# Projecting a cross-attention's context in four 32-row tiles of the array: keys and values of a Perceiver layer on Trainium2

## The chip, the cores and the metric

The kernel runs on one core of a Trainium2 chip, as one launch. The core has a matrix engine (TensorE; PE in the profile, with PEld for its weight loads), a vector engine (DVE), an activation engine (ACT), GpSimd (POOL) and an engine that issues transfers (SP). Matrix products are written into PSUM, which has eight banks of 128 partitions × 512 float32 numbers; the other engines read them from there. The metric is the device time of one execution in microseconds (us), lower is better. Times of a kernel are given as the median of several runs; the profile is of one further execution with a time of its own.

## The reference, cut to what matters

The program computes two layers of a Perceiver-like network on `x` (4 batches × 256 tokens × 256 channels) with a context `ctx` (4 × 4096 keys × 192 channels), all in float32:

```python
x = x + L0_xattn(layernorm(x), ctx, mask, Wq, Wk, Wv, Wo)     # the block that is changed
x = x + L0_attn(layernorm(x), ...)
x = x + L0_ffn(layernorm(x), ...)
x = x + L1_xattn(layernorm(x), ctx, ...)
x = x + L1_attn(layernorm(x), ...)
x = x + L1_ffn(layernorm(x), ...)
```

The block in question is an attention with 16 heads of 16 channels:

```python
q = (xn @ Wq).reshape(4, 256, 16, 16)      # Wq 256 x 256
k = (ctx @ Wk).reshape(4, 4096, 16, 16)    # Wk 192 x 256
v = (ctx @ Wv).reshape(4, 4096, 16, 16)    # Wv 192 x 256
p = softmax(where(mask, q . k / sqrt(16), -big))   # 256 x 4096 per batch and head
out = (p . v).reshape(4, 256, 256) @ Wo
```

The change touches the two products `ctx @ Wk` and `ctx @ Wv`: 4 × 4096 rows, 192 channels in, 256 out each.

## The kernel before, in words

`l0_xattn` works in 16 units, u = 4 × batch + g: four groups g of four heads for each of four batches. Four heads lie in the four 32-row groups of a tile (16 channels, then a row for the maximum, a row for the mask, padding). Keys `kts` and values `vs` each have two tiles, one for each pair of groups (`gp`): while one pair is read, the other is refilled. Between them lie 8 refills of keys and 8 of values (4 batches × 2 pairs), each in four chunks of 1024 keys.

A unit has 16 steps (`step`, lines 424 to 478). A step does two things side by side: for unit u it weighs 256 keys (`s`), and for the unit that is 18 steps (`LEAD`) ahead it looks for the largest score over a stretch of 512 keys (`a`). It has two half steps of two heads each. On TensorE a half step runs two `weigh(0)` matmuls (line 444, bank `ps_s`, 256 columns), two scores for the maximum (line 458, `ps_a`, 512 columns), two `weigh(1)`, and then `sums` (line 406), four matmuls of exponentials with values into `o_ps`. ACT takes the exponentials out of `ps_s` (line 469), DVE the maxima out of `ps_a` (line 473). `sums` uses the exponentials of the step before. In the profile every float32 matmul shows as two LDWEIGHTS and two MATMUL records.

PSUM: `x0_acc` holds one bank (`o_ps`), `x0_ring` the other seven, which `bank(name)` hands out in turn. A half step takes four: two `ps_s` and two `ps_a`. A bank can be written again when the engine that reads it is done.

The projections are generators, advanced by the loop at the end of `l0_xattn` after a step (line 508). `projections[u]` projects keys in even units and values in odd ones, for units 0 to 13. Keys advance by a chunk after steps 0, 4, 8 and 12 of their unit; values by half a chunk after every second step. Before the loop's first weighing there are 18 steps with `a` only, and in these the first refills (batch 0, pair 0) are done: keys up to step 3, values (`first_values`) half a chunk after each of steps 9 to 17, as far as there are any.

A keys chunk (`keys`, lines 288 to 309): a context chunk of 768 KB, laid out as 128 channels × 1024 keys and below it the other 64 channels as two halves of 512 keys, is loaded by `context_keys` (line 233) on SP's queue. Two banks get 512 keys each: two matmuls over 128 rows (line 295) and two over 64 rows, in the array's upper and lower half (line 298). ACT copies both banks to SBUF (line 301), and eight transfers of 64 KB spread the heads' rows into `kts` (line 305). Half a values chunk (`values`, lines 311 to 336): here the context is the stationary operand, with 128 keys to a matmul, and the weights (128 columns of one pair of groups) are streamed: four matmuls over 128 rows (line 322) and four over 64 rows (line 325) into two banks, in the order of two groups per 128 keys; ACT copies each bank (line 335) into `vs`.

Weights: `l0_xattn_weights` loads `x0_wk` by three transfers on ACT's queue (`load_kk`, lines 242 and 244) ahead of the first context chunk (line 200); `others`, called at step 3 of the first 18, loads `x0_wv`, the x rows of batches 1 to 3 (line 210) and `x0_wo` on SP. `tokens(b)` normalises a batch's x (`row_norm`, lines 120 to 134, DVE) and transposes it (line 347); `queries(u)` projects the queries of a unit, `with_largest(u)` puts the maxima into the query tile, `finish(u)` divides by the sum (`attn_finish`, lines 165 to 174) and after the fourth group adds the output projection.

The order on each engine follows the program text closely, but the framework that builds the program puts some instructions elsewhere: the trace shows the normalisation of batches 1 to 3 (line 127) at 29 to 36 us, long before the units that use it.

Of the kernel before, what the change touches and what calls it, by code (L numbers as in the profile page):

```python
# [11 lines left out]
F32 = mybir.dt.float32  # L12
# [9 lines left out]
P = 128  # L22
B, S, D = 4, 256, 256
# [96 lines left out]
def row_norm(c, pool, name, b):  # L120

    v = c.nc.vector
    xn = pool.tile([P, 2, D], F32, tag=name, name=name)
    mv = pool.tile([P, 2, 2], F32, tag="nr_mv", name="nr_mv")
    for i in range(2):
        st = pool.tile([P, 6], F32, tag="nr_st", name="nr_st")
        v.bn_stats(st, c.x[:, 2 * b + i, :])
        v.bn_aggr(mv[:, i, :], st)
    rs = newton_rsqrt(c, pool, mv[:, :, 1], 2)
    for i in range(2):  # L130
        v.tensor_scalar(
            xn[:, i, :], c.x[:, 2 * b + i, :], mv[:, i, 0:1], rs[:, i : i + 1], ALU.subtract, ALU.mult
        )
    return xn
# [60 lines left out]

def l0_xattn_weights(c, pool):
    w = Ctx()
    w.wk = load_kk(c, pool, "x0_wk", c.nc.scalar)
    w.ctxT = [pool.tile([P, 1536], F32, tag="ctxT0", name="ctxT0")]
    c.nc.scalar.dma_start(w.ctxT[0], c.a["ctxT"][0, 0])  # L200
    w.mu = pool.tile([64, S], U8, tag="mu", name="mu")
    c.nc.sync.dma_start(w.mu, c.a["gmask"].rearrange("b (a k) -> (b a) k", k=S))
    w.wq = load_k(c, pool, "x0_wq")

    def others():

        w.wv = load_kk(c, pool, "x0_wv")
        xv = c.a["x"].rearrange("b (t p) d -> p (b t) d", p=P)
        for i in range(2, NB, 2):
            c.nc.sync.dma_start(c.x[:, i : i + 2, :], xv[:, i : i + 2, :])  # L210
# [18 lines left out]
def context_keys(c, pool, b, c4, queue=None):  # L229


    t = pool.tile([P, 1536], F32, tag="ctxT", name="ctxT")
    (queue or c.nc.sync).dma_start(t, c.a["ctxT"][b, c4])
# [12 lines left out]


def l0_xattn(c, w):
# [5 lines left out]

    nc, tc = c.nc, c.tc
    W = 17
    LEAD = 18
    with ExitStack() as es:  # L260
# [5 lines left out]
        def bank(name):  # L266
            return ring.tile([P, 512], F32, tag="mm", name=name)

        kts, vs, mexps = [], [], []
        for i in range(2):  # L270
# [7 lines left out]
        w.ctxT += [context_keys(c, two, 0, 1), context_keys(c, two, 0, 2, nc.scalar)]  # L278
# [4 lines left out]
        def mask(b, gp):  # L283
            for i in range(2):
                nc.sync.dma_start(kts[gp][17:P:32, i, :], c.mrow[b].partition_broadcast(4))

        def keys(b, gp):

            gs = slice(gp * P, (gp + 1) * P)
            first = (b, gp) == (0, 0)  # L290
            for c4 in range(4):
                ctxT = w.ctxT.pop(0) if w.ctxT else context_keys(c, two, b, c4)
                pss = [bank("ps_k0"), bank("ps_k1")]
                for j, ps in enumerate(pss):
                    nc.tensor.matmul(ps, w.wk[:, 0, gs], ctxT[:, j * 512 : (j + 1) * 512], start=True, stop=False)
                for j, ps in enumerate(pss):
                    hs = slice(64 * j, 64 * j + 64)
                    nc.tensor.matmul(ps, w.wk[hs, 1, gs], ctxT[hs, 1024:1536], start=False, stop=True)  # L298
                ks = two.tile([P, 2, 512], F32, tag="ks", name="ks")
                for j, ps in enumerate(pss):  # L300
                    nc.scalar.copy(ks[:, j, :], ps)  # L301
                for i in range(2):
                    for h in range(4):
                        r = 64 * i + 16 * h
                        ((nc.scalar, nc.gpsimd)[i] if first else nc.sync).dma_start(
                            kts[gp][32 * h : 32 * h + 16, i, c4 * 1024 : (c4 + 1) * 1024],
                            ks[r : r + 16].rearrange("p j n -> p (j n)"),
                        )
                yield

        def values(b, gp):
            v = vs[gp]
            gs = slice(gp * P, (gp + 1) * P)
            for c4 in range(4):
                ctxT = context_keys(c, two, b, c4)
                for i0 in (0, 2):
                    pss = [bank("ps_v0"), bank("ps_v1")]
                    for i in (i0, i0 + 1):
                        ks = slice((i - i0) * P, (i - i0 + 1) * P)
                        for j, ps in enumerate(pss):  # L320
                            k0 = j * 512 + i * P
                            nc.tensor.matmul(ps[:, ks], ctxT[:, k0 : k0 + P], w.wv[:, 0, gs], start=True, stop=False)  # L322
                        for j, ps in enumerate(pss):
                            hs = slice(64 * j, 64 * j + 64)
                            nc.tensor.matmul(  # L325
                                ps[:, ks],
                                ctxT[hs, 1024 + i * P : 1024 + (i + 1) * P],
                                w.wv[hs, 1, gs],
                                start=False,
                                stop=True,  # L330
                            )
                    for j, ps in enumerate(pss):
                        n0 = (8 * c4 + 4 * j + i0) * 8
                        o = v[:, n0 * W : (n0 + 16) * W].rearrange("p (n d) -> p n d", d=W)
                        nc.scalar.copy(o[:, :, 0:16], ps[:, 0 : 2 * P].rearrange("p (n d) -> p n d", d=16))  # L335
                    yield

        xnTs = {}

        def tokens(b):  # L340

            xn = row_norm(c, two, "xn", b)
            xnT = two.tile([P, 2, S], F32, tag="xnT", name="xnT")
            ps = bank("ps_t")
            for k in range(2):
                for i in range(2):
                    nc.tensor.transpose(
                        ps[:, k * S + i * P : k * S + (i + 1) * P], xn[:, i, k * P : (k + 1) * P], c.ident
                    )
            nc.scalar.copy(xnT.rearrange("p k n -> p (k n)"), ps)  # L350
            xnTs[b] = xnT
# [66 lines left out]
        def finish(u):  # L418
            b, g = divmod(u, 4)
            on = one.tile([P, S], F32, tag=f"on{g}", name=f"on{g}")  # L420
            attn_finish(c, two, ring, o_pss.pop(u)[:, :S], on)
            ons.append(on)
            if g == 3:
                add_projected(c, ring, b, ons, w.wo)
                ons.clear()
# [58 lines left out]
        for t in range(-LEAD, n):  # L484
            if t < 0:
                i = t + LEAD
                if i in (0, 2):
                    next(first_keys, None)
                if i == 3:
                    w.others()  # L490
                    for j in range(2):
                        nc.gpsimd.memset(kts[1][:, j, :], 1.0)
                if i > 8:
                    next(first_values, None)
            u, kp = divmod(t, 16)
            ua, ka = divmod(t + LEAD, 16)
            if ua < 16 and ka == 0 and ua > 0:
                queries(ua)
            if ua < 15 and ka == 8 and ua % 4 == 3:
                tokens(ua // 4 + 1)  # L500
            step((u, kp) if t >= 0 else None, (ua, ka % 2, ka // 2) if ua < 16 else None)
            if ua < 16 and ka == 15:
                with_largest(ua)
            if u in projections:
                steps, nb, ngp = projections[u]
                if kp == 0 and u % 2 == 0:
                    mask(nb, ngp)
# [1445 lines left out]
def _arrays(i):  # L1953
# [11 lines left out]
    for m in range(P):  # L1965
# [18 lines left out]
        "x": i["x"],  # L1984
        "ctx": i["ctx_768"],
        "ctxT": ctxT,
        "gmask": i["mask_BxS2_bf1"].view(np.uint8),
        "cols": cols,
        "sel": sel,
        "x0_wq": _pad_cols(i["L0_xattn_Wq"], 16, 16, 32),  # L1990
        "x0_wk": i["L0_xattn_Wk"],
        "x0_wv": i["L0_xattn_Wv"],
# [74 lines left out]
```

## Time and profile before

| what | value |
|---|---|
| runs | 2672.73, 2675.63, 2672.99 us; median 2672.99 |
| profiled execution | 2677.02 us, its span 2674.9 us |
| mean granted TensorE clock over the span | 0.929 |
| TensorE busy | 2420.3 us, 90% of the span |
| DVE busy, ACT busy | 1618.9 us (61%), 1095.0 us (41%) |
| layer 0's cross-attention | 0 to about 1236 us |
| of this, TensorE busy from 250 to 1180 us | 908.7 of 930 us |
| first key projection, first max reduce, first o_ps | 10.41, 24.87, 103.22 us |

How to read it. A group line names the source line, the engine, the operation, what is written and what is read, their shapes and how many there were; behind the bar the sum of their durations (us), the mean of one (ns), and the idle time of the engine just before them with what ended it. A timeline line has the start (us), the duration, the engine and the line, and a count where neighbouring instructions of the same kind are drawn together. Durations of matmuls overlap, since they are pipelined: four matmuls side by side in the array show their full latency each. What a stretch of matmuls costs is read from where the next one starts. "32\*128 32x256" is an operand of 32 rows (a quarter of the array's rows) × 128 columns, with 256 columns streamed through it.

### The profile page before, as it was taken

To read this page: it belongs to the slowest core of one execution; us is meant where nothing else is said; L and a number is where in the kernel's file an instruction comes from. 1 tells how busy PE (TensorE), PEld (TensorE's weight loads), DVE (VectorE), ACT (ScalarE), POOL (GpSimd) and SP (SyncE) were. 2 spreads that over 40 slices of the span, in tenths; PEclk is the share of its full clock that TensorE was granted. 3 is DMA by queue.
4 is the path that set the end of the run, shared out by engine and by line. 5 is a ranking of instruction groups with operands and counts; after the bars stand their busy time and mean duration, and the time that the engine had idled before them with its cause. 6 is when DMAs were issued, how large, how long until landed. Compare 5 with 4: busy or idle time off the path is not lost. (4 is left out here: it accounts for less than half of the span.)

```text
span 2674.9 us, 47755 instructions
## 1 busy us (share of the span) xinstructions
PE 2420.3 (90%) x19345; PEld 1419.5 (53%) x19345; DVE 1618.9 (61%) x3881; ACT 1095.0 (41%) x1913; POOL 179.1 (7%) x202
## 2 busy tenths in 40 slices
PE   8999999999999999999768989888999898984896
PEld 4445454545545454544435544466776777453554
DVE  6655655565565655561784440898798892735554
ACT  1355555555455555556111211555555562010221
POOL 3000000000000000000030000001010011412000
PEclk7899999999999999999888999799999999996876
DMA  7221213121221212100100012210303012100110
GB/s 197 76 53 58 61 50 80 38 73 45 62 56 55 63 37 73 45 2 1 43 1 1 5 47 67 79 60 20 99 22 97 6 50 96 55 0 16 33 24 8
DMA packets 63186, 130.78 MB, mean 49 GB/s; under 512 B 11584, under 2 KB 38912, under 8 KB 62512
## 3 DMA queue, kind: packets, MB, share of 16 engines
q1 hardware_dynamic: 61344, 123.73, 16.4%
q8 instruction: 154, 2.52, 0.4%
q10 hardware_dynamic: 1104, 2.88, 0.4%
q0 software_dynamic: 512, 1.05, 0.2%
q14 instruction: 72, 0.59, 0.1%
HBM read 97.12 MB, written 5.34 MB: 38 GB/s over the span
## 5 line engine op out<-in xcount | busy, mean ns | idle before, releaser
L473 DVE TENSOR_REDUCE mx<-ps_a 128x1 f32<-128x512 f32 x1024 | 658.3, 686 | 436.1 <-PE ps_a L458 436.1
L469 ACT ACTIVATE e<-ps_s 128x512 f32<-128x512 f32 x1024 | 555.8, 594 | 382.5 <-PE ps_a L458 356.5
L458 PE MATMUL ps_a<-kt,qa 32*128 32x512 f32 x2048 | 636.2, 653 | 1.9 <-DMA kt<-ks 0.8
L444 PE MATMUL ps_s<-qb,kt 32*128 32x256 f32 x4096 | 585.9, 401 | 0.0
L444 PEld LDWEIGHTS ps_s<-qb,kt 32*128 32x128 f32 x4096 | 348.7, 184 | 212.4 <-issue 94.2
L406 PE MATMUL o_ps<-e,v 128*32 128x256 f32 x4096 | 327.6, 391 | 0.0
L1152 PEld LDWEIGHTS ps_w<-diag,e 128*128 128x128 f32 x2048 | 238.8, 197 | 23.5 <-issue 21.5
L1152 PE MATMUL ps_w<-diag,e 128*128 128x128 f32 x2048 | 244.5, 281 | 0.4 <-POOL diag L1139 0.4
L458 PEld LDWEIGHTS ps_a<-kt,qa 32*128 32x128 f32 x2048 | 220.6, 186 | 20.9 <-DVE mx L473 7.8
L1109 DVE MAX8 cand<-sc 128x8 f32<-128x128 f32 x1024 | 212.2, 275 | 8.7 <-ACT sc L1097 8.7
L406 PEld LDWEIGHTS o_ps<-e,v 128*32 128x32 f32 x4096 | 81.0, 108 | 239.5 <-issue 229.5
L1133 DVE SCALAR_TENSOR_TENSOR e<-sc,top,e 128x1024 f32<-128x1024 f32 x128 | 159.1, 1279 | 28.5 <-ACT e L1124 28.5
L1124 ACT ACTIVATE e<-sc,neg 128x1024 f32<-128x1024 f32 x128 | 143.1, 1147 | 33.3 <-PE ps_w L1152 29.1
L1097 ACT COPY sc<-ps_s 128x1024 f32<-128x1024 f32 x128 | 126.3, 1007 | 41.9 <-PE ps_s L1088 39.6
L1166 PEld LDWEIGHTS ps_c<-cx,wT 128*128 128x128 f32 x512 | 86.1, 196 | 27.2 <-ACT wT L1160 11.3
L1166 PE MATMUL ps_c<-cx,wT 128*128 128x193 f32 x512 | 97.1, 341 | 1.9 <-ACT wT L1160 1.9
L335 ACT COPY v<-ps_v 128x256 f32<-128x256 f32 x128 | 41.4, 375 | 137.0 <-PE ps_v L325 137.0
L322 PE MATMUL ps_v<-x_wv,ctxT 128*128 128x128 f32 x512 | 92.8, 305 | 0.0
L322 PEld LDWEIGHTS ps_v<-x_wv,ctxT 128*128 128x128 f32 x512 | 69.4, 195 | 35.3 <-DVE mx L473 21.8
L1088 PE MATMUL ps_s<-kt,q 32*128 32x512 f32 x512 | 85.4, 647 | 0.0
L889 POOL MEMSET s_low<- 128x128 f32 x2 | 0.3, 206 | 1241.1 <-DVE x L188 1241.1
L301 ACT COPY ks<-ps_k 128x512 f32<-128x512 f32 x64 | 34.4, 589 | 111.4 <-PE ps_k L298 97.7
(403 smaller groups left out, 2735.6 us busy)
## 6 DMA issues: line engine op xcount, KB each, us to landing
ctxT<-in_ctxT SPq DMA_DIRECT2D x78, 768.0 KB
kt<-ks SPq DMA_DIRECT2D x352, 64.0 KB
cx<-in_ctx SPq DMA_DIRECT2D x16, 768.0 KB
x_w<-in_x_w SPq DMA_DIRECT2D x2, 1024.0 KB
qk<-rot SPq DMA_DIRECT2D x8, 256.0 KB
a_qk<-qk SPq DMA_DIRECT2D x16, 128.0 KB
ctxT<-in_ctxT ACTq DMA_DIRECT2D x2, 768.0 KB
x<-in_x SPq DMA_DIRECT2D x4, 256.0 KB
```

What stands on the lines that cost most here:

```text
L322: nc.tensor.matmul(ps[:, ks], ctxT[:, k0 : k0 + P], w.wv[:, 0, gs], start=True, stop=False)
L406: nc.tensor.matmul(o_pss[u][32 * h : 32 * h + 32, :S], vs[g // 2][:, c0 : c0 + 32], ew[h][:, n % 2, :], start=(n == 0), stop=(n == GT - 1),)
L444: nc.tensor.matmul(ps[:, k * S : (k + 1) * S], kts[u % 4 // 2][hs, u % 2, ks], qbs[u][hs, :], start=True, stop=True,)
L458: nc.tensor.matmul(ps, qas[u][hs, tt * P : (tt + 1) * P], kts[u % 4 // 2][hs, u % 2, ch * 512 : (ch + 1) * 512], start=True, stop=True,)
L469: nc.scalar.activation(e, ps.rearrange("p (k n) -> p k n", k=2), AF.Exp)
L473: nc.vector.tensor_reduce(mxs[u][:, tt, h, ch : ch + 1], ps, AX.X, ALU.max)
L1097: nc.scalar.copy(t, ps)
L1109: nc.vector.max(cands[u][:, n, :], sc[u][c4][:, i // 4, (i % 4) * P : (i % 4 + 1) * P])
L1124: nc.scalar.activation(t, src, AF.Exp, bias=neg)
L1133: nc.vector.scalar_tensor_tensor(t, src, top[:, 31:32], t, ALU.is_ge, ALU.mult)
L1152: nc.tensor.matmul(ps[:, i * P : (i + 1) * P], e[c4][:, half, i * P : (i + 1) * P], diag, start=(h == 0), stop=(h == 3),)
L1166: nc.tensor.matmul(ps_c[:, : DC + 1], wT[:, i * P : (i + 1) * P], cxs[b][t][:, j, :], start=(n == 0), stop=(n == 31))
```

## The change

The 192 context channels are dealt out as six blocks of 32 instead of 128 + 64. A chunk of 1024 keys is laid out on the 128 partitions as four quarters of 256 keys, each on 32 partitions: partition 32 j + p holds channel 32 k + p of quarter j at place k (`ctx6`, 6 × 256 numbers on a partition, 768 KB in all as before). The weights lie in SBUF four times, once in each 32-partition group. Each channel block k is then multiplied for the four quarters in four row tiles of the array, which write into four PSUM banks, and six such rounds add up in each bank.

- Keys: 24 matmuls of 32 rows × 256 columns instead of 2 of 128 rows and 2 of 64 rows × 512 columns, for each chunk.
- Values: 48 matmuls of 32 rows × 128 columns instead of 8 and 8 for a chunk; a chunk is projected in one go, after steps 0, 4, 8 and 12 (`kp % 4 == 0` in both kinds of unit), in four banks. `first_values` advances after steps 9, 11, 13 and 15 of the first 18.
- Copies out of PSUM: four of 256 columns per chunk, two on ACT and two on DVE (all four on ACT for the first keys and values).
- Weight loads: the first pair's `wk` by four transfers of 96 KB on ACT's queue; the others, 12 transfers of 96 KB, on SP, ahead of the x rows.
- `xn`, `xnT` and the tiles of `attn_finish` come from the pool with one buffer instead of that with two.

```diff
-    w.wk = load_kk(c, pool, "x0_wk", c.nc.scalar)
-    w.ctxT = [pool.tile([P, 1536], F32, tag="ctxT0", name="ctxT0")]
-    c.nc.scalar.dma_start(w.ctxT[0], c.a["ctxT"][0, 0])
+    w.wk = pool.tile([P, 2, 6, P], F32, tag="x0_wk", name="x0_wk")
+    w.wv = pool.tile([P, 2, 6, P], F32, tag="x0_wv", name="x0_wv")
+    def part(t, name, gp, queue):
+        for r in range(4):
+            queue.dma_start(t[32 * r : 32 * r + 32, gp], c.a[name][gp])
+    part(w.wk, "x0_wk6", 0, c.nc.scalar)
+    w.ctxT = [pool.tile([P, 6, 256], F32, tag="ctxT0", name="ctxT0")]
+    c.nc.scalar.dma_start(w.ctxT[0], c.a["ctx6"][0, 0])
...
     def others():
-        w.wv = load_kk(c, pool, "x0_wv")
+        part(w.wv, "x0_wv6", 0, c.nc.sync)
+        part(w.wk, "x0_wk6", 1, c.nc.sync)
+        part(w.wv, "x0_wv6", 1, c.nc.sync)
...
+        def copy(j, out, ps, first):
+            if first or j < 2:
+                nc.scalar.copy(out, ps)
+            else:
+                nc.vector.tensor_copy(out, ps)
...
         def keys(b, gp):
...
-                pss = [bank("ps_k0"), bank("ps_k1")]
+                pss = [bank("ps_k") for _ in range(4)]
+                for k in range(6):
+                    for j, ps in enumerate(pss):
+                        hs = slice(32 * j, 32 * j + 32)
+                        nc.tensor.matmul(ps[:, :256], w.wk[hs, gp, k, :], ctxT[hs, k, :], start=(k == 0), stop=(k == 5))
+                ks = two.tile([P, 1024], F32, tag="ks", name="ks")
                 for j, ps in enumerate(pss):
-                    nc.tensor.matmul(ps, w.wk[:, 0, gs], ctxT[:, j * 512 : (j + 1) * 512], start=True, stop=False)
-                for j, ps in enumerate(pss):
-                    hs = slice(64 * j, 64 * j + 64)
-                    nc.tensor.matmul(ps, w.wk[hs, 1, gs], ctxT[hs, 1024:1536], start=False, stop=True)
...
+                    copy(j, ks[:, j * 256 : (j + 1) * 256], ps[:, :256], first)
...
         def values(b, gp):
             for c4 in range(4):
-                for i0 in (0, 2):
-                    pss = [bank("ps_v0"), bank("ps_v1")]
...
+                pss = [bank("ps_v") for _ in range(4)]
+                for i in range(2):
+                    ks = slice(i * P, (i + 1) * P)
+                    for k in range(6):
                         for j, ps in enumerate(pss):
+                            hs = slice(32 * j, 32 * j + 32)
+                            nc.tensor.matmul(ps[:, ks], ctxT[hs, k, ks], w.wv[hs, gp, k, :], start=(k == 0), stop=(k == 5))
+                for j, ps in enumerate(pss):
+                    n0 = (8 * c4 + 2 * j) * 8
+                    o = v[:, n0 * W : (n0 + 16) * W].rearrange("p (n d) -> p n d", d=W)
+                    copy(j, o[:, :, 0:16], ps[:, :256].rearrange("p (n d) -> p n d", d=16), (b, gp) == (0, 0))
+                yield
...
-            xn = row_norm(c, two, "xn", b)
-            xnT = two.tile([P, 2, S], F32, tag="xnT", name="xnT")
+            xn = row_norm(c, one, "xn", b)
+            xnT = one.tile([P, 2, S], F32, tag="xnT", name="xnT")
...
-            attn_finish(c, two, ring, o_pss.pop(u)[:, :S], on)
+            attn_finish(c, one, ring, o_pss.pop(u)[:, :S], on)
...
-                if i > 8:
+                if i > 8 and i % 2:
                     next(first_values, None)
...
-                if kp % 2 == 0 if u % 2 else kp % 4 == 0:
+                if kp % 4 == 0:
                     next(steps, None)
```

More of the change, by code (lines that the diff above doesn't have):

```diff
@@ L277, in l0_xattn, with context @@
             mexps.append(m)
-        w.ctxT += [context_keys(c, two, 0, 1), context_keys(c, two, 0, 2, nc.scalar)]
+        def context(b, c4, queue=nc.sync):
+            t = two.tile([P, 6, 256], F32, tag="ctxT", name="ctxT")
+            queue.dma_start(t, c.a["ctx6"][b, c4])
+            return t
+        w.ctxT += [context(0, 1), context(0, 2, nc.scalar)]
         nc.gpsimd.memset(kts[0][:, 0, :], 1.0)
@@ L285, in mask @@
                 nc.sync.dma_start(kts[gp][17:P:32, i, :], c.mrow[b].partition_broadcast(4))
+        def copy(j, out, ps, first):
[3 more added lines that the diff above has]
+                nc.vector.tensor_copy(out, ps)
         def keys(b, gp):
-            gs = slice(gp * P, (gp + 1) * P)
             first = (b, gp) == (0, 0)
             for c4 in range(4):
-                ctxT = w.ctxT.pop(0) if w.ctxT else context_keys(c, two, b, c4)
-                pss = [bank("ps_k0"), bank("ps_k1")]
-                for j, ps in enumerate(pss):
-                    nc.tensor.matmul(ps, w.wk[:, 0, gs], ctxT[:, j * 512 : (j + 1) * 512], start=True, stop=False)
-                for j, ps in enumerate(pss):
-                    hs = slice(64 * j, 64 * j + 64)
[L298 to L301, printed above, removed]
+                ctxT = w.ctxT.pop(0) if w.ctxT else context(b, c4)
+                pss = [bank("ps_k") for _ in range(4)]
[4 more added lines that the diff above has]
+                ks = two.tile([P, 1024], F32, tag="ks", name="ks")
+                for j, ps in enumerate(pss):
+                    copy(j, ks[:, j * 256 : (j + 1) * 256], ps[:, :256], first)
                 for i in range(2):
@@ L305, in keys @@
                         ((nc.scalar, nc.gpsimd)[i] if first else nc.sync).dma_start(
[L306 to L307 removed]
+                            kts[gp][32 * h : 32 * h + 16, i, c4 * 1024 : (c4 + 1) * 1024], ks[r : r + 16]
                         )
@@ L312, in values @@
             v = vs[gp]
-            gs = slice(gp * P, (gp + 1) * P)
             for c4 in range(4):
-                ctxT = context_keys(c, two, b, c4)
-                for i0 in (0, 2):
-                    pss = [bank("ps_v0"), bank("ps_v1")]
-                    for i in (i0, i0 + 1):
-                        ks = slice((i - i0) * P, (i - i0 + 1) * P)
-                        for j, ps in enumerate(pss):
[L321 to L336, printed above, removed]
@@ new lines, in values @@
+                ctxT = context(b, c4)
+                pss = [bank("ps_v") for _ in range(4)]
+                for i in range(2):
+                    ks = slice(i * P, (i + 1) * P)
+                    for k in range(6):
+                        for j, ps in enumerate(pss):
+                            hs = slice(32 * j, 32 * j + 32)
[4 more added lines that the diff above has]
+                    copy(j, o[:, :, 0:16], ps[:, :256].rearrange("p (n d) -> p n d", d=16), (b, gp) == (0, 0))
@@ L1986, in _arrays @@
         "ctxT": ctxT,
+        "ctx6": i["ctx_768"].reshape(B, 4, 4, 256, 6, 32).transpose(0, 1, 2, 5, 4, 3).reshape(B, 4, P, 6, 256),
         "gmask": i["mask_BxS2_bf1"].view(np.uint8),
@@ L1990, in _arrays @@
         "x0_wq": _pad_cols(i["L0_xattn_Wq"], 16, 16, 32),
-        "x0_wk": i["L0_xattn_Wk"],
-        "x0_wv": i["L0_xattn_Wv"],
+        "x0_wk6": i["L0_xattn_Wk"].reshape(6, 32, 2, P).transpose(2, 1, 0, 3),
+        "x0_wv6": i["L0_xattn_Wv"].reshape(6, 32, 2, P).transpose(2, 1, 0, 3),
         "x0_wo": _pad_cols(i["L0_xattn_Wo"].T, 16, 16, 32).T,
```

## The prediction

> **What bounds the kernel now.** I read the page's engine totals first, then the busy time by stretch, the groups of instructions, and last the timeline of single steps in the middle of the stage that the change touches. That stage, layer 0's cross-attention, runs from the start to about 1232 us. The totals, and its stretch from 250 to 1180 us (busy PE, PEld, DVE, ACT, POOL, then the granted TensorE clock, DMA share and GB/s):
>
> ```profile
> PE 2420.3 (90%) x19345; PEld 1419.5 (53%) x19345; DVE 1618.9 (61%) x3881; ACT 1095.0 (41%) x1913; POOL 179.1 (7%) x202
> ...
> 250.00:1180.00 930.00, 908.68 (x8957) 468.34 (x8955) 549.20 (x853) 486.17 (x942) 0.00 (x0) 1.00 0.20 55
> ```
>
> TensorE is busy for 98% of the stretch at full clock, DVE for 59%, ACT for 52%, DMA for 20%. So TensorE time is what counts here. The groups of the projections, up to 1210 us:
>
> ```profile
> L322 PE MATMUL ps_v<-x_wv,ctxT 128*128 128x128 f32 x512 | 92.8, 305 | 0.0
> ...
> L295 PE MATMUL ps_k<-ctxT,x_wk 128*128 128x512 f32 x128 | 67.5, 653 | 10.4 <-DMA ctxT<-in_ctxT 10.4
> L325 PE MATMUL ps_v<-x_wv,ctxT 64*128 64x128 f32 x512 | 64.3, 328 | 0.0
> L335 ACT COPY v<-ps_v 128x256 f32<-128x256 f32 x128 | 41.4, 375 | 137.0 <-PE ps_v L325 137.0
> ...
> L298 PE MATMUL ps_k<-ctxT,x_wk 64*128 64x512 f32 x128 | 37.3, 660 | 0.0
> L301 ACT COPY ks<-ps_k 128x512 f32<-128x512 f32 x64 | 34.4, 589 | 111.4 <-PE ps_k L298 97.7 <-PE ps_a L458 8.0 <-DMA x<-in_x 5.7
> ```
>
> Each written matmul has two records (two passes, each with a weight load), so 128 records of L295 are 32 chunks of 4. A mean of 653 ns holds latency too; the price of a pass is the spacing of starts, for which the timeline serves. A keys chunk and half a values chunk:
>
> ```profile
> 606.43 0.64 PE L406 MATMUL o_ps<-e,v 128*32 128x256 f32 x8
> 607.00 1.98 PE L295 MATMUL ps_k<-ctxT,x_wk 128*128 128x512 f32 x4
> 608.92 1.13 PE L298 MATMUL ps_k<-ctxT,x_wk 64*128 64x512 f32 x4
> 609.98 0.48 PE L444 MATMUL ps_s<-qb,kt 32*128 32x256 f32 x2
> ```
> ```profile
> 683.55 0.71 PE L322 MATMUL ps_v<-x_wv,ctxT 128*128 128x128 f32 x4
> 684.20 0.49 PE L325 MATMUL ps_v<-x_wv,ctxT 64*128 64x128 f32 x4
> 684.62 0.71 PE L322 MATMUL ps_v<-x_wv,ctxT 128*128 128x128 f32 x4
> 685.26 0.49 PE L325 MATMUL ps_v<-x_wv,ctxT 64*128 64x128 f32 x4
> 685.68 0.48 PE L444 MATMUL ps_s<-qb,kt 32*128 32x256 f32 x2
> ```
>
> Keys hold TensorE for 609.98 − 607.00 = 2.98 us, half a values chunk for 685.68 − 683.55 = 2.13, so a whole one for 4.26. From one o_ps to the same one a step later, a plain step takes 3.54 us, one with keys 6.51 (+2.97), one with half a values chunk 5.66 (+2.12). The 28 keys chunks and 28 values chunks of the main loop so cost 28 × (2.97 + 4.24) = 202 us. Beside them PSUM banks matter, as a plain step shows:
>
> ```profile
> 601.58 0.95 PE L458 MATMUL ps_a<-kt,qa 32*128 32x512 f32 x2
> ...
> 602.12 0.59 PE L458 MATMUL ps_a<-kt,qa 32*128 32x512 f32 x1
> 602.32 0.38 PE L444 MATMUL ps_s<-qb,kt 32*128 32x256 f32 x2
> 602.38 0.59 PE L458 MATMUL ps_a<-kt,qa 32*128 32x512 f32 x1
> ```
>
> The two ps_a, which elsewhere start together, are 0.26 us apart: the second waits for its ring bank until DVE has reduced an earlier ps_a. That is why the half steps last 1.64 and 1.90 us.
>
> **Price of the new passes.** Keys after: 6 channel blocks × 2 passes of 256 columns, four row tiles side by side. Individual records at 600.25, .46 and .68 show 216 ns per such pass; a first pass comes 107 ns after its exposed weight load. So 0.107 + 12 × 0.216 = 2.70 us against 2.97. Before, two 128-row groups and two 64-row groups already shared the array (8 passes of 428 ns, of which the 64-row ones run in pairs: 6 × 428 = 2.57), and the rest was the change between the two tilings, about 0.1 us, which goes.
>
> Values after: 2 × 6 × 2 = 24 passes of 128 columns. Records of a later stage (L612, four row tiles, at 1558.29, .40 and .51) show 110 ns; the 128-row passes of L322 have 112. So 0.107 + 24 × 0.110 = 2.75 us against 4.24. The streaming itself hardly changes: before, a whole chunk had 16 passes of 128 rows and 8 of two 64-row tiles, 24 × 112 = 2.69 us. What goes is the eight starts of a group in another tiling, (4.24 − 2.69) / 8 = 0.19 us each, of which one is left.
>
> **A rule against it.** Side by side, 96 pairs of weight load and matmul must be handed to the array in 2.64 us, 27.5 ns each. The trace has 8 pairs at that pace (the L612 ones: 221 ns), but no long run: a later stage's densest is
>
> ```profile
> 1324.95 0.86 PE L632 MATMUL ps_w<-p,kn 128*32 128x256 f32 x16
> ```
>
> 54 ns each, and there 256-column passes and waits set the pace. The Trainium skill, "TensorE: Matmul & The Clock Gate", section "Wait — 56ns, not 53.3ns?", says that the start-to-start never falls below about 25 ns, and that with hardware decode off each matmul takes about 62 ns to issue. By 62, values would take 5.95 us and keys 2.98; by the row, 2.64 and 2.59. Eight starts at 27.6 ns are direct evidence against 62, unless a queue filled ahead feeds a short burst, so I take 27.5 and keep 62 as the upper bound.
>
> **Banks after it.** Seven ring banks are handed out in order. A half step takes four and a projection now four instead of two. Followed through the order of allocation: the projection's four get banks of the last step (released in time or under its own first passes), the next half step's ps_s and first ps_a too, but its second ps_a gets the projection's first bank and waits for that bank's ACT copy. Before, no bank of a projection came up before the half step after that. With T the end of the projection's stream: last passes drain 0.16, semaphore to ACT 0.03, copy 0.375 (L335), back to TensorE 0.055: ps_a starts at T + 0.62 instead of about T + 0.01. From ps_a to o_ps is 1.05 us, from o_ps to the next half step 0.57: that half step ends at T + 2.24 instead of 1.64. The following one then meets no wait (1.64, not 1.90), because DVE has caught up. So the step after the stream takes 3.88, not 3.54: +0.34 per projection. "TensorEngine Tiling (Array Packing)", section "Gotcha 1: PSUM Pressure", warns of this, each row tile having its own bank; here it has the price 0.34 us.
>
> **Sum of the main loop.** Keys: 2.70 + 0.34 = 3.04 against 2.97: +0.07 × 28 = +2 us. Values: 2.75 + 0.34 = 3.09 for one chunk and one stall, since chunks are no longer halved, against 4.24: −1.15 × 28 = −32 us. Together −30.
>
> Two of four copies go to DVE, 128 × 256 from PSUM: 425 ns (L391) to 484 (L377), so about 0.9 us per chunk. A step with a chunk has 2.6 us of reduces in 6.6 us: 3 us of DVE idle cover it; without that cover it would be 56 × 0.9 = 50 us. ACT loses 2 × 589 or 4 × 375 and gains 2 × 375: nothing, as it isn't the bound. The context loads keep their size (768 KB) and number, and the eight 64 KB kt transfers per keys chunk stay, on SP.
>
> **Start.** Here the change adds. Weights now lie in SBUF four times. On ACT's queue the first wk half becomes four DMAs (384 KB in place of 256 in three) ahead of ctxT chunk 0, which releases the first matmul at 10.41 us: +131 KB at the 216 GB/s of the first 40 us is +0.6 us. On SP, 12 DMAs of 96 KB replace three, and stand ahead of:
>
> ```profile
> 19.60 0.34 SPq L233 DMA_DIRECT2D ctxT<-in_ctxT  x1
> 20.52 3.50 SPq L210 DMA_DIRECT2D x<-in_x  x3
> ```
>
> Nine more issues and 0.9 MB more (4 us at 216 GB/s) put these 2 to 6 us back. Behind them: the fourth keys chunk (30.41), and by the built order the statistics of x for batches 1 to 3, which now stand on DVE ahead of the first max reduce:
>
> ```profile
> 24.87 0.69 DVE L473 TENSOR_REDUCE mx<-ps_a 128x1 f32<-128x512 f32 x1 [3.75 <-PE ps_a L458]
> ```
>
> That reduce waits for x rows till about 31 to 33: 6 to 8 us late, with all scores behind it, as their banks wait for DVE. DVE is busy for only 24.7 of the first 40 us, so I count on some 4 us of this being made up. First values: four chunks in eight steps, bound by DVE's reduces, ring waits in between; PE gains its 1.5 us per chunk but a two-step cycle has 5.2 us of reduces plus copies and waits, about 7.1 against 6.4 now, +2.8 in all. I take +5 us, from −3 (all hidden, PE's gain kept) to +12.
>
> Norm tiles xn and xnT have one buffer in place of two: at one place in unit 3 some 3 us of small norm operations fall between reduces: 0 to +4, taken as +2. attn_finish's tiles with one buffer: a unit is 60 us long, so nothing.
>
> **Total:** −30 + 5 + 2 = −23. The profiled execution took 2677.02 with a span of 2674.9, 2.1 outside the span: span 2652, profiled 2654. The median of the runs is 4.0 below the profiled one: 2650.
>
> **Rivals.** (1) TensorE's instruction supply becomes the bound. Its price is 28 × (96p − 2.64 us) for a pair time p, and above 54 ns keys' 48 pairs add too. It decides from 23 / 28 = 0.82 us per chunk, p = 36 ns. At 45 ns: +47, total +24, 2697; at 62 ns: +93 + 11, total +81, 2754. For it: no run of 96 pairs at 27 ns in the trace, and 17% more pairs (19,345 + 32 × 40 + 32 × 64 = 22,673). Against it: the 8 starts. It ends slower.
> (2) Waits eat the gain. If DVE is late with the projection's two copies or ps_a waits 0.3 us longer than worked out, 56 × 0.3 = +17; or the start costs 12 and more. Then −10 to +5: 2663 to 2678, about no change. For it: four of seven banks tied up; against it: DVE idles 40%.
> (3) The stall of 0.34 doesn't show: −19 more, 2631. Against it: the order of the ring is fixed.
>
> **How the numbers follow.** Likeliest case 0.63 (its own range 2635 to 2663), rival 1 0.20, rival 2 0.12, rival 3 0.05. A measurement tells 0.2%, 5.3 us, from no change. Faster: 0.63 + 0.05 + 0.03 of rival 2 = 0.71; same 0.06; slower 0.20 + 0.03 = 0.23. The range leaves out rival 1's paces beyond about 46 ns (0.13) and the bottom end: 2626 to 2700.
>
> **What would show it.** Starts of the new key passes 216 ns apart, of value passes 110: groups of 2.7 us each between o_ps and ps_s. Value groups of 4 us or more are rival 1. After each chunk, the second ps_a 0.6 us behind the first, released by ACT's copy; steps of 6.58 and 6.63 us, plain ones 3.54. Start: first max reduce at 31 to 33, first o_ps about 108 where it was at 103.2. The forecast is wrong if steps with values come out over 7.4 us or the first o_ps after 120.

## The result, and the profile after

The changed kernel takes 2657.55 us (median of five runs, 2650.49 to 2663.63) against 2672.96 before (2671.63 to 2675.63): ratio 0.9939, 95% interval 0.9917 to 0.9962, or 15.4 us less. On another chip it was 2661.03 against 2678.49 (0.9927, 0.9906 to 0.9948). The forecast was 2650, in a range of 2626 to 2700. The profiled execution has a span of 2661.6 us, 13.3 less than before. The stage that is changed, layer 0's cross-attention, ends in it at 1265.2 us, and before the change at 1275.5: the 1236 and 1232 us given for it ahead of the result are too early.

The engine totals and the stretch from 250 to 1180 us of the changed kernel:

```profile
PE 2390.3 (90%) x22673; PEld 1453.8 (55%) x22673; DVE 1671.0 (63%) x3993; ACT 1064.9 (40%) x1865; POOL 178.8 (7%) x202
...
250.00:1180.00 930.00, 904.44 (x11626) 493.35 (x11619) 603.76 (x985) 470.53 (x913) 0.00 (x0) 1.00 0.21 55
```

TensorE has 3,328 more matmul records and is busy 30 us less. DVE has gained the copies, ACT has lost some. The groups up to 1210 us that take the place of L295 to L335:

```profile
L342 PE MATMUL ps_v<-x_wv,ctxT 32*128 32x128 f32 x3072 | 107.8, 280 | 0.9
L320 PE MATMUL ps_k<-ctxT,x_wk 32*128 32x256 f32 x1536 | 106.1, 399 | 13.1 <-DMA ctxT<-in_ctx 13.1
...
L307 ACT COPY v<-ps_v 128x256 f32<-128x256 f32 x72 | 22.9, 378 | 110.8 <-PE ps_v L342 110.8
L309 DVE COPY v<-ps_v 128x256 f32<-128x256 f32 x56 | 21.2, 419 | 53.3 <-PE ps_v L342 53.3
L309 DVE COPY ks<-ps_k 128x256 f32<-128x256 f32 x56 | 21.1, 419 | 57.6 <-issue 31.0 <-PE ps_k L320 24.1 <-ACT ks L307 2.6
```

The means (280 and 399 ns) say little, since four matmuls run side by side. A values chunk and what follows it, in the timeline:

```profile
500.15 0.64 PE L417 MATMUL o_ps<-e,v 128*32 128x256 f32 x8
...
500.72 3.11 PE L342 MATMUL ps_v<-x_wv,ctxT 32*128 32x128 f32 x95
...
503.56 0.38 PE L455 MATMUL ps_s<-qb,kt 32*128 32x256 f32 x2
...
503.76 0.65 ACT L307 COPY v<-ps_v 128x256 f32<-128x256 f32 x2 [2.29 <-PE ps_v L342]
503.85 0.76 DVE L309 COPY v<-ps_v 128x256 f32<-128x256 f32 x2 [2.31 <-PE ps_v L342]
...
504.19 0.18 PEld L469 LDWEIGHTS ps_a<-kt,qa 32*128 32x128 f32 x1 [0.42 <-ACT v L307]
...
505.24 0.64 PE L417 MATMUL o_ps<-e,v 128*32 128x256 f32 x8
```

The chunk holds TensorE from 500.72 to 503.56, 2.84 us. The second ps_a behind it is released by ACT's copy and loads its weights at 504.19, 0.63 after the stream; the next o_ps is 5.09 us behind the last. In the single records, the starts of one row tile lie 111 or 112 ns apart from the fourth of the 24 passes to the last. With four tiles side by side that is 28 ns for each pair of weight load and matmul, 96 pairs in a chunk. A keys chunk:

```profile
574.62 2.91 PE L320 MATMUL ps_k<-ctxT,x_wk 32*128 32x256 f32 x47
...
577.31 0.38 PE L455 MATMUL ps_s<-qb,kt 32*128 32x256 f32 x2
...
577.93 0.18 PEld L469 LDWEIGHTS ps_a<-kt,qa 32*128 32x128 f32 x1 [0.42 <-ACT ks L307]
```

The stream takes 2.69 us with passes 216 ns apart, and again 0.62 pass from its end to the second ps_a. The half step behind it then lasts 1.64 us where it was 1.90 before: one ring wait of 0.26, which every plain step has, is absorbed.

The start is where the change lost. SP's issue of the x rows, the first of them used by DVE after its wait, and the first max reduce:

```profile
27.52 2.39 SPq L220 DMA_DIRECT2D x<-in_x  x3
...
34.96 0.43 DVE L127 BATCH_NORM_STATS2 nr_st<-x 128x6 f32<-128x256 f32 x1 [11.26 <-DMA x<-in_x]
...
43.38 0.69 DVE L484 TENSOR_REDUCE mx<-ps_a 128x1 f32<-128x512 f32 x1
```

The x rows went out 7 us later than before, DVE stood 11.3 us waiting for them, and the first max reduce came at 43.4 us in place of 24.9. TensorE waited 9.7 us for it (a ps_a at 44.12). The first o_ps came at 113.4 us instead of 103.2.

### The profile page after: what moved, and what is told of

Same layout as the page of the kernel before. It is cut to its first block, busy times and chain, and to the rows that moved or that the text cites. A ratio compares the mean times of both kernels' runs of the same rounds, so it can differ in the third digit from the quotient of the medians.

```text
span 2661.6 us, 54614 instructions
## 1 busy us (share of the span) xinstructions
PE 2390.3 (90%) x22673; PEld 1453.8 (55%) x22673; DVE 1671.0 (63%) x3993; ACT 1064.9 (40%) x1865; POOL 178.8 (7%) x202
## 3 DMA queue, kind: packets, MB, share of 16 engines
q0 software_dynamic: 512, 1.05, 0.2%
## 5 line engine op out<-in xcount | busy, mean ns | idle before, releaser
L469 PE MATMUL ps_a<-kt,qa 32*128 32x512 f32 x2048 | 658.1, 647 | 13.7 <-DVE mx L484 9.8
L455 PE MATMUL ps_s<-qb,kt 32*128 32x256 f32 x4096 | 595.2, 401 | 0.0
L469 PEld LDWEIGHTS ps_a<-kt,qa 32*128 32x128 f32 x2048 | 229.7, 186 | 56.1 <-DVE mx L484 18.3
L320 PE MATMUL ps_k<-ctxT,x_wk 32*128 32x256 f32 x1536 | 106.1, 399 | 13.1 <-DMA ctxT<-in_ctx 13.1
L342 PE MATMUL ps_v<-x_wv,ctxT 32*128 32x128 f32 x3072 | 107.8, 280 | 0.9
L342 PEld LDWEIGHTS ps_v<-x_wv,ctxT 32*128 32x128 f32 x3072 | 100.0, 191 | 15.3 <-issue 11.0
L320 PEld LDWEIGHTS ps_k<-ctxT,x_wk 32*128 32x128 f32 x1536 | 89.7, 193 | 27.0 <-issue 23.9
L1177 PEld LDWEIGHTS ps_c<-cx,wT 128*128 128x128 f32 x512 | 86.1, 196 | 27.2 <-ACT wT L1171 11.3
```

The lines of the kernel that those rows point to most:

```text
L320: nc.tensor.matmul(ps[:, :256], w.wk[hs, gp, k, :], ctxT[hs, k, :], start=(k == 0), stop=(k == 5))
L342: nc.tensor.matmul(ps[:, ks], ctxT[hs, k, ks], w.wv[hs, gp, k, :], start=(k == 0), stop=(k == 5))
L455: nc.tensor.matmul(ps[:, k * S : (k + 1) * S], kts[u % 4 // 2][hs, u % 2, ks], qbs[u][hs, :], start=True, stop=True,)
L469: nc.tensor.matmul(ps, qas[u][hs, tt * P : (tt + 1) * P], kts[u % 4 // 2][hs, u % 2, ch * 512 : (ch + 1) * 512], start=True, stop=True,)
L1177: nc.tensor.matmul(ps_c[:, : DC + 1], wT[:, i * P : (i + 1) * P], cxs[b][t][:, j, :], start=(n == 0), stop=(n == 31))
```

## The experiments

Measured from each profile, by the starts of o_ps as in the prediction: the first max reduce, the first o_ps, the stretch from the first o_ps to that of unit 14 (which holds 27 of the 28 keys chunks, as one lies ahead of the first o_ps, and all 28 values chunks), the step with a keys and with a values chunk, and the rest of the program behind the last o_ps of the stage. The last columns are the medians and the ratio to the kernel before, run on the same chip.

| kernel | first max reduce | first o_ps | to unit 14 | keys step | values step | rest | median | ratio (95%) |
|---|---|---|---|---|---|---|---|---|
| before | 24.9 | 103.2 | 1063.4 | 6.51 | 5.66 (half) | 1399.4 | 2672.96 | |
| changed | 43.4 | 113.4 | 1042.9 | 6.58 | 6.73 | 1396.4 | 2657.55 | 0.9939 (0.9917 to 0.9962) |
| after_again | 40.6 | 110.0 | 1042.9 | 6.58 | 6.73 | 1399.5 | 2661.03 | 0.9927 (0.9906 to 0.9948) |
| keys_only | 32.3 | 108.0 | 1069.9 | 6.58 | 5.66 (half) | 1389.1 | 2678.06 | 1.0026 (1.0010 to 1.0041) |
| values_only | 24.8 | 105.5 | 1038.5 | 6.51 | 6.73 | 1394.8 | 2648.00 | 0.9913 (0.9879 to 0.9946) |
| act_copies | 41.7 | 113.4 | 1042.9 | 6.58 | 6.73 | 1388.7 | 2651.64 | 0.9934 (0.9901 to 0.9967) |
| split_copy | 41.6 | 113.6 | 1053.5 | 6.80 | 6.90 | 1392.9 | 2670.80 (one run) | |
| x_first | 27.1 | 100.1 | 1042.9 | 6.58 | 6.73 | 1387.0 | 2641.41 | 0.9852 (0.9806 to 0.9898) |
| rows64 | 26.7 | 103.9 | 1024.4 | 6.31 | 6.41 | | 2629.14 | 0.9802 (0.9757 to 0.9847) |
| rows64_two | 24.4 | 100.3 | 1022.2 | 6.31 | 6.41 | 1382.5 | 2624.83 | 0.9802 (0.9756 to 0.9849) |
| rows64_x_first | 27.8 | 97.7 | 1022.2 | 6.31 | 6.41 | 1399.0 | 2621.93 | 0.9812 (0.9780 to 0.9844) |

The stretch to unit 14 repeats within 0.1 us from execution to execution, so it tells apart what the total, which moves by ten, can't.

**after_again.** The changed kernel, unaltered.

> The changed kernel once more, unaltered: its five runs lie between 2650.5 and 2663.6 us, a spread of 13 us where the kernel before has 4. If the spread comes from the start (weight transfers, context and x rows sharing the DMA queues), the first o_ps moves within about 105 to 116 us (113.4 in the first profile) while the stretch from there to unit 14's first o_ps stays at 1043.0 us within 1. If it comes from the stages behind, the first o_ps is 113 again and the stretch after 1230 us moves.

Both came: the first o_ps moved to 110.0 and the stretch stayed, but the rest moved too, by 3 us here and by up to 17 over all kernels (below). In these two profiles the total moves at the start and behind the stage, and not in the changed steps.

**Keys alone and values alone.** Each takes the other projection, its loads, layout and schedule from the kernel before. For keys_only:

```diff
         def values(b, gp):
...
+                ctxT = context_keys(c, two, b, c4)
+                for i0 in (0, 2):
+                    pss = [bank("ps_v0"), bank("ps_v1")]
...
-                if kp % 4 == 0:
+                if kp % 2 == 0 if u % 2 else kp % 4 == 0:
```

> Keys in the new layout, values as before (half chunks, 128 and 64 rows, two banks). If the sum is right for keys, the stretch from the first o_ps to unit 14's (1063.4 us before) grows: steps with keys 6.58 in place of 6.51, 0.4 at each odd unit's end, 1.9 in unit 2 for the single-buffered norm: 1.5 + 2.9 + 1.9 = about 6 us, to 1069 or 1070; with a later start of 3 to 8 us the whole is 8 to 14 us slower than before. If the new keys are worth something by themselves, steps come below 6.51.

> Values in the new layout, keys as before. If all of the gain is in the values, the stretch from the first o_ps to unit 14's takes about 1043.0 - 1.5 - 2.9 = 1038 to 1039 us, 25 less than before and 4 to 5 less than with both; the first matmul is back at 10.4 us (wk not replicated), the first o_ps at 105 to 110; about 20 us faster than before, 5 to 8 faster than the full change. If keys and values gain from each other (one layout, one context tile), the stretch is 1043 or more.

The stretches came out at 1069.9 and 1038.5, as worked out. Keys in the new layout lose: 6.4 us in the loop, 4.8 at the start. Values gain 25 us in the loop. Against the forecasts, keys_only is 4.7 us slower than before, not 8 to 14, and values_only 25 faster, not 20: the rest of the program was 10 and 5 us shorter in their profiles than in that of before, in stages that the change doesn't touch (last section). By the totals values_only (0.9913) and the full change (0.9939) aren't told apart, their intervals overlap; the stage ends at 1252.8 us with values alone and at 1265.2 and 1261.8 with both.

**act_copies.** All four copies on ACT:

```diff
-            if first or j < 2:
-                nc.scalar.copy(out, ps)
-            else:
-                nc.vector.tensor_copy(out, ps)
+            nc.scalar.copy(out, ps)
```

> The changed kernel with all four copies of a projection on ACT. If the copies on DVE lie wholly in its idle time, as the sum has it, steps stay at 6.58 and 6.73 within 0.05 and the time within 3 us of the changed kernel. If the two copies on DVE hold up its reduces, steps fall by 0.2 or more (10 us in all). If ACT can't take four copies in a row in time for the half step that reuses banks three and four, they grow by 0.2 to 0.5 (11 to 28 us).

Steps and stretch are the same to 0.02 us, while DVE's busy time from 250 to 1180 us falls from 603.8 to 568.4:

```profile
250.00:1180.00 930.00, 904.46 (x11626) 493.37 (x11619) 568.39 (x889) 497.19 (x1009) 0.00 (x0) 1.00 0.21 55
```

So the copies on DVE cost nothing and bring nothing. The ratio of 0.9934 is the changed kernel's too (0.9939 and 0.9927), and the stage ends at 1265.2 us in both profiles.

**split_copy.** The copy of each projection's first bank shared by ACT and DVE (shown for keys; values in the same halves):

```diff
+            if j == 0 and not first:
+                nc.scalar.copy(out[:, :128], ps[:, :128])
+                nc.vector.tensor_copy(out[:, 128:], ps[:, 128:])
+            elif first or j < 3:
+                nc.scalar.copy(out, ps)
```

> The changed kernel with the copy of each projection's first bank shared: 128 columns on ACT, 128 on DVE at the same time; banks two and three are then copied by ACT, four by DVE. If the second ps_a behind a chunk waits for the first bank's copy, it comes earlier by what the copy is shorter: 256 columns take 375 ns on ACT, 512 take 589, so 128 about 268 (an estimate from these two), steps of 6.58 and 6.73 shrink by 0.05 to 0.11 us, to about 6.50 and 6.65, and the stretch from the first o_ps to unit 14's from 1042.9 to 1037 to 1040. If the wait is for something else (DVE's reduces, the array's own drain), the steps stay at 6.58 and 6.73 within 0.02, or grow, as DVE has more to do there.

Steps grew by 0.2 us. The timeline (at a unit's end, where the same waits hold) shows why:

```profile
564.87 0.27 ACT L308 COPY ks<-ps_k 128x128 f32<-128x128 f32 x1 [3.57 <-PE ps_k L327]
...
565.17 0.29 DVE L309 COPY ks<-ps_k 128x128 f32<-128x128 f32 x1 [0.79 <-ACT ks L308]
...
565.51 0.18 PEld L476 LDWEIGHTS ps_a<-kt,qa 32*128 32x128 f32 x1 [0.64 <-DVE ks L309]
565.52 0.70 PE L462 MATMUL ps_s<-qb,kt 32*128 32x256 f32 x4
```

The halves weren't taken at the same time: DVE's was released by ACT's. The bank came free at 565.46 instead of 0.375 after 564.87, at 565.25, 0.21 us later; the waiting ps_a, released by DVE's half, loaded its weights 0.05 after that, and the ps_s queued behind it started at 565.52. Steps grew by about the same (6.58 to 6.80; 6.73 to 6.90), the stretch by 10.6 us, 0.19 for each of its 55 chunks. The experiment missed its sign, since the first bank was freed later instead of sooner, and yet tells the theories apart: the step moves with the release of the first bank. Why the built program made DVE wait wasn't tried.

**x_first.** In `others`, the three loads of x rows ahead of the twelve of weights.

```diff
     def others():
+        xv = c.a["x"].rearrange("b (t p) d -> p (b t) d", p=P)
+        for i in range(2, NB, 2):
+            c.nc.sync.dma_start(c.x[:, i : i + 2, :], xv[:, i : i + 2, :])
         part(w.wv, "x0_wv6", 0, c.nc.sync)
         part(w.wk, "x0_wk6", 1, c.nc.sync)
         part(w.wv, "x0_wv6", 1, c.nc.sync)
-        xv = c.a["x"].rearrange("b (t p) d -> p (b t) d", p=P)
...
```

> Only the order of the loads in others() is changed: the x rows of batches 1 to 3 go out ahead of the twelve weight transfers. If the order on SP's queue is what delays the first max reduce to 43 us (DVE waits 11.3 us for x rows at 35 us), the reduce comes by about 30, the first o_ps at 105 to 108 instead of 113.4, and the whole is 5 to 8 us faster than the changed kernel. If the transfers as such (1.2 MB of replicated weights in the first 40 us) are the limit, the order is worth nothing: first o_ps 111 to 115, the time within 3 us.

```profile
10.42 1.09 SPq L217 DMA_DIRECT2D x<-in_x  x2
...
16.23 0.42 DVE L127 BATCH_NORM_STATS2 nr_st<-x 128x6 f32<-128x256 f32 x1
...
27.09 0.69 DVE L484 TENSOR_REDUCE mx<-ps_a 128x1 f32<-128x512 f32 x1 [2.27 <-PE ps_a L469]
```

The x rows go out 17 us earlier, DVE finishes the norms while TensorE projects the first keys, and the first max reduce comes at 27.1. The first o_ps comes at 100.1, more than was expected: 10 to 13 earlier than in the two profiles of the changed kernel and 3 earlier than before the change, although the first projection still starts at 12.9 us and the same bytes are moved. So the order on one queue, not the bytes, made the loss at the start. The median fell by 19.6 us against after_again. Of the 22.4 us between the two profiled spans only 9.9 lie in the stage, the other 12.5 in the rest, which the edit doesn't touch.

A late x row alone does not delay the reduces, as values_only shows. There eight weight transfers stand ahead of the x rows, which go out even later than in the changed kernel, and yet the first max reduce comes as early as before the change, because the built program has the norms behind it on DVE:

```profile
24.78 0.69 DVE L485 TENSOR_REDUCE mx<-ps_a 128x1 f32<-128x512 f32 x1 [4.24 <-PE ps_a L470]
...
29.32 2.96 SPq L218 DMA_DIRECT2D x<-in_x  x3
...
38.68 0.42 DVE L127 BATCH_NORM_STATS2 nr_st<-x 128x6 f32<-128x256 f32 x1
```

In these profiles it takes both: the x rows late on the queue, and their norms ahead of the reduces on DVE. No run moved the norms alone.

**rows64, rows64_two, rows64_x_first.** The same idea with tiles of 64 rows: three blocks of 64 channels, two halves of 512 keys in two banks.

```diff
-                pss = [bank("ps_k") for _ in range(4)]
-                for k in range(6):
+                pss = [bank("ps_k") for _ in range(2)]
+                for k in range(3):
                     for j, ps in enumerate(pss):
-                        hs = slice(32 * j, 32 * j + 32)
-                        nc.tensor.matmul(ps[:, :256], w.wk[hs, gp, k, :], ctxT[hs, k, :], start=(k == 0), stop=(k == 5))
+                        hs = slice(64 * j, 64 * j + 64)
+                        nc.tensor.matmul(ps, w.wk[hs, gp, k, :], ctxT[hs, k, :], start=(k == 0), stop=(k == 2))
```

> The same idea with 64-row tiles: three blocks of 64 channels, two halves of 512 keys in two row tiles, two PSUM banks in place of four; as many passes, weights in SBUF twice instead of four times, a values chunk still in one go, both copies (512 columns) on ACT. If the four banks cause the wait behind each chunk (second ps_a released by ACT's first copy), it is gone: keys steps 3.54 + 2.70 = 6.24 us in place of 6.58, values steps about 6.30 in place of 6.73, some 0.3 less at each unit end; 28 x 0.34 + 28 x 0.43 + 14 x 0.3 = 26 us, and 2 to 5 at the start: 2626 to 2635. If the wait is DVE's or comes from the longer chunk, steps stay at 6.5 to 6.7 and the time within 5 us of the changed kernel's.

> As rows64, with xn, xnT and the attn_finish tiles in two buffers again (the smaller weights leave room). If the single buffer puts the norm of batch 2 among the reduces of unit 2 (5.45 us for a step of 3.54 there), that step is 3.54 again, and the first 120 us gain up to 3 us since the norms no longer stand on DVE ahead of the reduces: 2 to 5 us faster than rows64. If not, the two are equal within 2 us.

> Two 64-row tiles, two buffers for the norm, and the x rows ahead of the weights in others(). If the x rows' place in SP's queue still delays the start, the first o_ps comes at 95 to 98 us instead of 100.3, 2 to 5 us faster in all. If the two buffers had already taken DVE's wait away, the first o_ps stays within 1 us of 100.3. The stretch from there to unit 14's first o_ps stays at 1022.1.

A keys chunk of rows64_two:

```profile
585.94 2.85 PE L320 MATMUL ps_k<-ctxT,x_wk 64*128 64x512 f32 x12
...
588.72 0.48 PE L455 MATMUL ps_s<-qb,kt 32*128 32x256 f32 x2
588.73 0.19 PEld L469 LDWEIGHTS ps_a<-kt,qa 32*128 32x128 f32 x2
588.73 0.70 PE L469 MATMUL ps_a<-kt,qa 32*128 32x512 f32 x2
...
589.79 0.64 PE L417 MATMUL o_ps<-e,v 128*32 128x256 f32 x8
```

Both ps_a start together, 0.01 us after the first ps_s: with two banks to a projection the wait is gone. A keys step is 6.31, 3.54 + 2.78 to 0.01; the 32-row one is 3.54 + 2.69 + 0.35. The stream itself is 0.09 longer than with 32 rows, and the single records show where: from its last pass to the 32-row ps_s behind it 0.52 us pass, while its passes of 512 columns lie 0.43 apart. I read this as the change of tiling, which the 32-row stream doesn't have there; it had been left out, so steps are 6.31 and 6.41 where 6.24 and 6.30 were expected. The stretch is 18.6 us shorter than the changed kernel's with four banks. (The profile of rows64 has a granted clock of 0.50 from 1177 to 1286 us, across the end of the stage; its rest is left out of the table.) Two buffers for the norm take the 5.67 us of one step in unit 2 back to 3.54 and the first o_ps from 103.9 to 100.3, as expected. With the x rows first it is 97.7. These versions beat both kernels: 2621.93 and 2624.83 us against 2673.39 and 2678.49 before on their chips, a ratio of 0.981 and 0.980; between the two the totals don't decide.

## Why the prediction was right, and where it wasn't

It forecast −23 us in the span, of which −30 in the loop, +2 for the norm and +5 at the start; the span shows −13.3. Term by term, from the profiles:

| step of the sum | forecast | measured |
|---|---|---|
| values: (2.75 + 0.34 − 4.24) × 28 | −32 | 3 × 3.54 + 6.73 against 2 × (3.54 + 5.66): −1.05 × 28 = −29.4 |
| keys: (2.70 + 0.34 − 2.97) × 28 | +2 | 6.58 − 6.51 = +0.07, × 27 in the stretch = +1.9 |
| norm with one buffer | +2 | 5.45 − 3.54 in unit 2 (not 3): +1.9 |
| attn_finish, the ends of units | 0 | 1042.95 − 1063.43 = −20.5, less the three above: +5.1 |
| start | +5 | 113.4 − 103.2 = +10.2 (+6.8 in the second profile) |
| behind the stage | 0 | 1396.4 − 1399.4 = −3.0 |

**Right: the price of the passes, and rival 1.** Passes start 216 and 112 ns apart, and a chunk of 96 pairs runs at 28 ns a pair. The bound of 62 ns, which the Trainium skill gives for issue without hardware decode ("TensorE: Matmul & The Clock Gate", "Wait — 56ns, not 53.3ns?"), doesn't hold here. Its floor of about 25 ns from start to start is kept by the mean of 28, not by single starts: those of the four tiles of one pass lie 7 ns apart. Short bursts in the trace of before had been enough to tell.

**Right: the banks.** The wait was forecast at T + 0.62 and is at T + 0.62 and 0.63, released by the copy named. rows64 (two banks: no wait) and split_copy (first bank free 0.21 later: steps 0.2 longer) show that it hangs on the first bank. Without it, by the sum, 32-row keys would gain 0.27 per chunk instead of losing 0.07. Rival 3, that it wouldn't show, fell. Of rival 2's two halves, waits and start, the second came in part; DVE's copies, its first suspect, cost nothing (act_copies).

**Mis-sized: values.** −1.05 in place of −1.15. The stream is 2.84, not 2.75: 112 ns a pass instead of 110 (0.05), and at the second pass about 0.06 of idle, since the fourth tile's bank was still being reduced by DVE when the other three began. I had counted on that wait being hidden.

**Left out: the ends of units.** The sum took the price of a chunk in the middle of a unit 28 times. With attn_finish's tiles in one buffer nothing waits, as said, but a chunk at a unit's end costs about 0.4 us more than elsewhere, and 13 of them lie in the stretch. The larger part lies just ahead of it. Each chunk's bank wait absorbs a ring wait of 0.26, but the chunk after step 12 doesn't keep this gain: behind it TensorE waits, once a unit, for DVE's maxima to put them into a query tile (`ps_m`), and now waits longer by just that much. Before, and changed:

```profile
614.39 0.44 PE L389 MATMUL ps_m<-ident,mexp 128*128 128x128 f32 x2 [0.80 <-DVE mexp L384]
```
```profile
617.30 0.44 PE L400 MATMUL ps_m<-ident,mexp 128*128 128x128 f32 x2 [1.06 <-DVE mexp L395]
```

The half step with it takes 4.71 us instead of 4.45, so that it and the one ahead of it are 6.35 in both kernels. The other runs agree: in values_only the wait is 1.06 behind values and 0.80 behind keys, in keys_only the other way round, and in rows64_two, which has no bank wait, 0.80 behind both. The smaller part, read from keys, is the chunk at the end itself, which used to follow `den` (the sums that a unit is divided by) in the same 128-row tiling. Before, and changed:

```profile
554.61 0.70 PE L171 MATMUL den<-o_sb,sel 128*128 128x256 f32 x2 [0.97 <-ACT o_sb L169]
...
555.14 1.88 PE L295 MATMUL ps_k<-ctxT,x_wk 128*128 128x512 f32 x4
...
558.01 0.48 PE L444 MATMUL ps_s<-qb,kt 32*128 32x256 f32 x2
```
```profile
556.80 0.70 PE L171 MATMUL den<-o_sb,sel 128*128 128x256 f32 x2 [0.97 <-ACT o_sb L169]
...
557.42 2.87 PE L320 MATMUL ps_k<-ctxT,x_wk 32*128 32x256 f32 x48
...
560.12 0.38 PE L455 MATMUL ps_s<-qb,kt 32*128 32x256 f32 x2
```

The old keys chunk began 0.53 us behind `den` and took 2.87, 0.10 less than in the middle of a unit; the new one begins 0.62 behind it and takes 2.69, as in the middle. That is about 0.2 of gain that isn't there, and rows64_two, without any bank wait, misses it too: its keys gain 0.20 on the old ones in the middle (6.31 against 6.51) and nothing at the ends (7.92, as the old ones in values_only).

**Mis-sized: the start.** The step was right in kind (twelve transfers ahead of the x rows, the norms ahead of the max reduces on DVE) and half the size. I put the issue at 2 to 6 us late and the first reduce at 31 to 33. The issue was 7 late, the first rows could be used only 7.4 us after it, the norms then took DVE until the reduce at 43.4. The first projection, put at 0.6 us late, started 2.7 late (13.1 us against 10.4), but x_first, with 12.9, shows that this did not decide. That the late rows did is shown by x_first too, which takes the whole loss back and more.

One remark of the prediction doesn't add up, though no term of the sum rests on it: the old keys chunk's 2.97 less 2.57 for its passes leaves 0.40, of which a first pass at 0.107 stays, so that the change between its tilings was worth about 0.29, not 0.1.

For the span the forecast was 9.7 us too low: 5.1 from the ends of units, 5.2 from the start, 2.6 from the values, less the 3.0 behind the stage and 0.2 from keys and norm; for the median 7.6. The 3.0 behind the stage are luck: two executions of the changed kernel differ there by 3.1.

## What to carry to other kernels

When narrower tiles run side by side, each with a PSUM bank of its own as here, follow the order of the ring to find which later matmul gets the first of them, for it waits for that bank's copy; two 64-row tiles streamed as many columns here with half the banks and took 19 us less in the loop. A price per chunk read in the middle of a loop doesn't hold at its seams, where another wait can take back what the new one absorbed. Transfers added to a queue delay what stands behind them, and the scheduler may have put work that needs it ahead of the work that matters: moving three loads ahead of twelve was worth 10 us here, half of what the whole change gained in the loop.

## What the runs showed that I had not expected

The stages behind the attention, which no kernel here touches, took from 1382.5 to 1399.5 us, with the same instructions. From the end of the stage to the end, changed kernel and rows64_two:

```profile
1265.20:2661.60 1396.40, 1185.45 (x7635) 784.61 (x7635) 890.34 (x2698) 455.99 (x677) 158.12 (x171) 0.88 0.14 40
```
```profile
1231.30:2613.70 1382.40, 1171.58 (x7635) 777.57 (x7635) 889.67 (x2698) 455.84 (x677) 163.27 (x171) 0.89 0.14 40
```

DVE and ACT were busy for the same time to 0.7 us, TensorE for 14 us less, at a granted clock of 0.89 instead of 0.88; rows64_x_first, with 1399.0, had 1189.41 and 0.87. In the clock records of the traces the clock there goes down to 0.50 for stretches of 3 to 38 us, in part at other places in each execution; they add up to 334 us for the changed kernel and 303 for rows64_two, at half clock a difference of 15.6 us. Whether a shift in the start decides where they fall, or chance does, wasn't tried. With a rest that moves by more than ten microseconds, it was the stretch inside the stage, steady to 0.1 us, that decided between theories.
